# Four-layer convolution kernel: the sums of the last mixing's thresholded terms move from VectorE to GpSimd

## The chip, the core and the metric

The kernel runs on one core of one Trainium2 chip. The core has TensorE (PE in the profile), VectorE (DVE), ScalarE (ACT), GpSimd (POOL) and SyncE (SP), each with its own in-order stream of instructions, and a set of DMA engines fed by queues. The metric is the device time of one execution in microseconds (us).

## The reference

The input is four images of 64 channels of 256 x 256, all float32. Four layers follow each other. Layers 0, 1 and 3 convolve every channel with a filter that is a product of a row filter and a column filter, so that each is two products with Toeplitz matrices, and add `x * bias`. Layer 2 is the one that the change touches:

```python
f1 = haar2d(x)                                     # wavelet transform in both directions
for i in range(2):
    f4 = einsum('bchw,oc->bohw', f1 * v[i], conv_w[i])        # mixes the channels at each place
    acc = acc + sign(f4) * relu(abs(f4) - tau[i])             # a soft threshold
y = haar2d(acc, inverse=True) + x
```

## The kernel before, in words

For each image `b` the kernel runs layers 0 and 1 and the forward transform channel by channel (`convolutions`), then mixes the channels (`mixing`), then does the inverse transform and layer 3 channel by channel (`inverse`). The stages of one image are overlaid with those of the next. While the last image (b = 3) is mixed there is no next image; there the kernel does the layer 3 convolutions of 63 channels of the earlier images that were put off (`convolution`; their data come from the DRAM tensor `late`, and their steps carry the prefix "l").

The mixing of one image goes through 64 groups; a group holds 4 rows of the transform. Its steps, with their lines:

- `load` (L431, L435): a DMA fetches the group's coefficients `f`, and, for every fourth group, the scale factors `vt`.
- `mix` (L449): four matmuls (eight in the records) into `px` in PSUM.
- `scaled` (L468, VectorE) and `scaled_too` (L473, ScalarE): `f4 = px * v`. In the last mixing VectorE takes 8 of the 16 parts in one instruction, and ScalarE the other 8 one by one.
- `size` (L477, ScalarE): `mag = |f4|`. `sign` (L480, ScalarE): `f4 = sign(f4)`.
- `shrink` (L484, VectorE): `mag = mag - tau`. `signed` (L488, VectorE): `mag = max(mag, 0) * f4`.
- `add` (L494): two instructions, each of which adds the two terms i = 0, 1 of two of the rows and writes them into `z`, 256 elements for each of the 128 partitions.

`f4` and `mag` have two buffers each (pool `mx`, bufs=2). So L477 of group g + 2 overwrites what `add` of group g reads, and has to wait for it.

Two more kinds of work on VectorE lie in the same stretch. L292 is the sum at the end of a put-off convolution (`y = v * bias + product in PSUM`). L299 and L300 (`halve`, called by `level` and `butterfly`) are the levels of the inverse transform along one axis, done in place on `z`; the large ones take 128x1024 elements. A level needs the rows of `z` that it combines, and the channels 16 and up of `inverse` need the levels of their chunk of `z`.

The order on every engine is made when the program is built. Each step is put on a list with a due time (`at`, table `PLACE`), the list is sorted, and the framework then reorders instructions engine by engine by a cost model of its own, keeping the due times as priorities. An instruction whose inputs that model takes for ready can so be pulled ahead of others into what it takes for idle time. Waits between engines are semaphores set by the framework. On chip the order is fixed.

GpSimd does only one thing in this kernel: the short levels of the forward transform (L350 and L351 with lengths 32 to 2), 64 lots of ten instructions.

Of the kernel before, what the change touches and what calls it, by code (L numbers as in the profile page):

```python
# [16 lines left out]
B, C, S, EMB, ORD = 4, 64, 256, 33, 64  # L17
# [80 lines left out]
def conv_seq_kernel(ctx, tc, x, fz, fw, bias, decay, haar, haar_row, factors, vt, taut, wmix, out):  # L98
# [14 lines left out]
    nc = tc.nc  # L113
# [22 lines left out]
    z = zpool.tile([P, 4, P, 4, 16], F32, name="z")  # L136
# [182 lines left out]
    def at(time, run, unit):  # L319
        events.append((time, len(events), run, unit))  # L320
# [104 lines left out]
    def mixing(b, start, n_act):  # L425

        st = {}

        def load(g):
            f = mx.tile([P, 2, S], F32, name=f"f_{b}_{g}", tag="f", bufs=3)  # L430
            nc.sync.dma_start(f, coef[b].rearrange("k c p w -> (k c) p w")[:, 2 * g : 2 * g + 2])  # L431
            st[g] = {"f": f}
            if g % GT == 0:
                t = mx.tile([P, 2, GT, 16], F32, name=f"vt_{b}_{g}", tag="vt")
                nc.sync.dma_start(t, scales[g // GT])  # L435
                st["vt", g // GT] = t

        def scale(g, i):
            return st["vt", g // GT][:, i, g % GT, :]

        def over(g, i, n):
            return scale(g, i)[:, :n].unsqueeze(2).to_broadcast([P, n, C])

        def mix(g):
            f = st[g]["f"]
            ps = psx.tile([P, 2, 2, S], F32, name=f"px_{b}_{g}", tag="mix")
            for q in range(2):
                for h in range(2):
                    nc.tensor.matmul(  # L449
                        ps[:, q, h, :],  # L450
                        f[:, q, h * P : (h + 1) * P],
                        wb.rearrange("p r n -> p (r n)"),
                        start=True,
                        stop=True,
                    )
            if g == 0:

                one, two = ps[:, 0, :, :P], ps[:, 0, :, P:]
                d = mx.tile([P, 2, P], F32, name=f"d_{b}", tag="mag")
                nc.vector.tensor_copy(d, two)  # L460
                nc.vector.tensor_sub(two, one, d)
                nc.vector.tensor_add(one, one, d)
            st[g]["f4"] = mx.tile([P, 16, C], F32, name=f"f4_{b}_{g}", tag="f4")
            st[g]["px"] = ps.rearrange("p q h (r i o) -> p (q h r i) o", r=2, i=2)

        def scaled(g):
            px, n = st[g]["px"], 16 - n_act
            nc.vector.tensor_tensor(st[g]["f4"][:, :n], px[:, :n], over(g, 0, n), ALU.mult)  # L468

        def scaled_too(g, half):  # L470
            px, f4 = st[g]["px"], st[g]["f4"]
            for j in range(16 - n_act + half * (n_act // 2), 16 - (1 - half) * (n_act - n_act // 2)):
                nc.scalar.mul(f4[:, j], px[:, j], scale(g, 0)[:, j : j + 1])  # L473

        def size(g):
            mag = st[g]["mag"] = mx.tile([P, 16, C], F32, name=f"mag_{b}_{g}", tag="mag")
            nc.scalar.activation(mag, st[g]["f4"], AF.Abs)  # L477

        def sign(g):
            nc.scalar.activation(st[g]["f4"], st[g]["f4"], AF.Sign)  # L480

        def shrink(g):
            mag = st[g]["mag"]
            nc.vector.tensor_sub(mag, mag, over(g, 1, 16))  # L484

        def signed(g):
            mag = st[g]["mag"]
            nc.vector.scalar_tensor_tensor(mag, mag, 0.0, st[g]["f4"], ALU.max, ALU.mult)  # L488

        def add(g):  # L490
            parts = st.pop(g)["mag"].rearrange("p (q x i) (n c) -> p q i x n c", q=2, i=2, n=4)
            for q in range(2):
                to = slot(2 * g + q)
                nc.vector.tensor_add(  # L494
                    z[:, :, to].rearrange("p n x c -> p x n c"), parts[:, q, 0], parts[:, q, 1]
                )


        for g in range(S // 4):
            for name, stage in zip(  # L500
                ("mix load", "mix", "scaled", "scaled too", "scaled rest", "size", "sign", "shrink", "signed", "add"),
                (
                    load,
                    mix,
                    scaled,
                    lambda g: scaled_too(g, 0),
                    lambda g: scaled_too(g, 1),
                    size,
                    sign,
                    shrink,  # L510
                    signed,
                    add,
                ),
            ):
                at(start + g + PLACE[name if b + 1 < B else "l " + name], stage, g)
# [168 lines left out]
def slot(i):  # L684

    if i == 0:
        return 0
    n = 1 << i.bit_length() - 1
    return (2 * (i - n) + 1) * (P // 2 // n)
# [104 lines left out]
```

## Time and profile before

| What | us |
|---|---|
| median of 3 runs (lowest to highest) | 2875.76 (2874.41 to 2878.55) |
| the profiled execution | 2874.07 |
| its span in the trace | 2872.3 |
| PE busy | 2827.1 (98%) |
| DVE busy | 2494.9 (87%) |
| ACT busy | 2080.3 (72%) |
| POOL busy | 334.4 (12%) |

All times given as positions are from the start of the span. The last mixing's L488 instructions start between 2364.52 (group 0) and 2636.42 (group 63); GpSimd's last instruction starts at 2211.6. In a view in order of time a line gives the start, the time taken, engine, line, operation, output and inputs, size, and in brackets the engine's idle time before it with the instruction that ended it. The records of successive instructions of one engine overlap a little, so the time an instruction costs its engine is read from one start to the next.

### The profile page before, as it was taken

How to read it: one execution, taken by the hardware profiler on the slowest of the kernel's cores; microseconds unless marked ns; L12 is line 12 of the kernel's file. 1: busy time of each engine (PE TensorE's matmuls, PEld its weight loads, DVE VectorE, ACT ScalarE, POOL GpSimd, SP SyncE). 2: the span in 40 equal slices, each digit the busy share in tenths (PEclk: the TensorE clock that was granted, in tenths of full speed). 3: DMA queues.
4: the chain of work that ended last, by engine and by line, in shares of the span. 5: the costliest groups of instructions: out<-in, count | busy, mean ns of one | idle time of the engine just before them, and what ended most of it. 6: DMA issues, size and time to landing. Idle time of an engine off the chain costs nothing. (4 is left out here: it accounts for less than half of the span.)

```text
span 2872.3 us, 52434 instructions
## 1 busy us (share of the span) xinstructions
PE 2827.1 (98%) x16592; PEld 2555.6 (89%) x16592; DVE 2494.9 (87%) x4255; ACT 2080.3 (72%) x4950; POOL 334.4 (12%) x644
## 2 busy tenths in 40 slices
PE   9999999999999999999999999999999999999999
PEld 7899998898888898998898998998898998888998
DVE  4655558999999779999999779999999779999985
ACT  2333338999995558998985658999995659998554
POOL 0111111121121001221221001121121000000000
PEclk9999999999999999999999999999999999999999
DMA  6878787776667986777777986777777988787786
GB/s 182 249 231 230 232 232 227 207 208 204 205 209 213 289 254 198 214 213 214 209 207 236 299 255 196 213 214 216 208 208 235 297 266 235 229 238 212 224 241 201
DMA packets 599367, 649.77 MB, mean 226 GB/s; under 512 B 48465, under 2 KB 517044, under 8 KB 598964
## 3 DMA queue, kind: packets, MB, share of 16 engines
q1 hardware_dynamic: 536996, 578.61, 68.9%
q10 hardware_dynamic: 62096, 67.82, 6.7%
q8 instruction: 134, 2.20, 0.3%
q14 instruction: 141, 1.16, 0.1%
HBM read 426.77 MB, written 219.48 MB: 225 GB/s over the span
## 5 line engine op out<-in xcount | busy, mean ns | idle before, releaser
L261 PE MATMUL py<-t,a 128*128 128x256 f32 x3072 | 922.5, 382 | 9.5 <-ACT a L275 8.7
L275 ACT COPY a<-pa 128x512 f32<-128x512 f32 x768 | 478.8, 623 | 498.6 <-PE pa L262 455.2
L473 ACT ACTIVATE f<-px,vt 128x64 f32<-128x64 f32 x2816 | 610.5, 367 | 101.6 <-DVE f L468 101.1
L262 PEld LDWEIGHTS py<-t,a 128*128 128x128 f32 x3072 | 583.4, 190 | 79.3
L262 PE MATMUL py<-t,a 128*128 128x128 f32 x3072 | 590.0, 274 | 0.0
L261 PEld LDWEIGHTS py<-t,a 128*128 128x128 f32 x3072 | 497.3, 191 | 51.2 <-ACT a L275 19.0
L449 PE MATMUL px<-wb,f 128*128 128x256 f32 x2048 | 487.6, 380 | 7.6 <-ACT f L473 7.6
L449 PEld LDWEIGHTS px<-wb,f 128*128 128x128 f32 x2048 | 369.0, 190 | 50.0 <-ACT f L473 10.5
L351 POOL TENSOR_TENSOR sd<-less 128x128 f32<-128x128 f32 (+4 forms) x320 | 190.8, 596 | 1858.7 <-DVE less L350 1519.9
L534 ACT COPY zc<-z 128x512 f32<-128x512 f32 x256 | 282.1, 1105 | 108.1 <-PE pw L542 99.0
L484 DVE TENSOR_TENSOR mag<-mag,vt 128x1024 f32<-128x1024 f32 x256 | 316.6, 1237 | 12.3 <-ACT mag L477 11.5
L488 DVE SCALAR_TENSOR_TENSOR mag<-mag,f 128x1024 f32<-128x1024 f32 x256 | 316.6, 1238 | 0.0
L261 PE MATMUL pa<-t,y 128*128 128x256 f32 x1024 | 309.1, 384 | 6.8 <-DVE y L292 5.2
L261 PE MATMUL pa<-t,x 128*128 128x256 f32 x1024 | 305.9, 381 | 0.5 <-DMA t<-pad 0.5
L477 ACT ACTIVATE mag<-f 128x1024 f32<-128x1024 f32 x256 | 295.7, 1155 | 2.8 <-DVE z L494 0.4
L374 DVE TENSOR_TENSOR sp<-sd,sp 128x512 fp32r<-128x512 f32 x256 | 179.8, 702 | 129.3 <-ACT sp L369 128.2
L480 ACT ACTIVATE f<-f 128x1024 f32<-128x1024 f32 x256 | 285.8, 1116 | 3.5
L261 PE MATMUL pa<-t,u 128*128 128x256 f32 x772 | 233.2, 384 | 6.5 <-ACT w L548 2.8
L292 DVE SCALAR_TENSOR_TENSOR y<-x,bsb,py 128x512 f32<-128x512 f32 x256 | 190.9, 746 | 41.9 <-PE py L262 41.0
L262 PEld LDWEIGHTS pa<-t,x 128*128 128x128 f32 x1024 | 194.6, 190 | 26.3
L262 PEld LDWEIGHTS pa<-t,y 128*128 128x128 f32 x1024 | 194.5, 190 | 26.3
L292 DVE SCALAR_TENSOR_TENSOR y<-y,bsb,py 128x512 f32<-128x512 f32 x256 | 190.7, 745 | 26.0 <-PE py L262 25.6
(73 smaller groups left out, 4412.3 us busy)
## 6 DMA issues: line engine op xcount, KB each, us to landing
t<-pad SPq DMA_DIRECT2D x768, 256.0 KB, 4.1
x<-in_x SPq DMA_DIRECT2D x256, 256.0 KB, 3.7
coef<-co SPq DMA_DIRECT2D x256, 256.0 KB, 3.2
f<-coef SPq DMA_DIRECT2D x256, 256.0 KB, 3.2
r<-keep SPq DMA_DIRECT2D x256, 256.0 KB, 4.1
out_y<-y ACTq DMA_DIRECT2D x193, 256.0 KB, 4.3
keep<-sums SPq DMA_DIRECT2D x256, 128.0 KB, 2.8
keep<-sd SPq DMA_DIRECT2D x256, 128.0 KB, 2.8
```

The lines of the kernel that those rows point to most:

```text
L261: nc.tensor.matmul(ps[:, m, :], src[:, 0, m * P : (m + 1) * P], t[:, ::-1], start=True, stop=False)
L262: nc.tensor.matmul(ps[:, m, P:], src[:, 1, m * P : (m + 1) * P], t[:, : P - 1 : -1], start=False, stop=True)
L275: nc.scalar.copy(a, s["p" + new])
L292: nc.vector.scalar_tensor_tensor(y, s[res], bsb[:, layer, c : c + 1], s["p" + new], ALU.mult, ALU.add)
L351: engine.tensor_tensor(t[:, :, :, half:length], v[..., 0], v[..., 1], ALU.subtract)
L449: nc.tensor.matmul(ps[:, q, h, :], f[:, q, h * P : (h + 1) * P], wb.rearrange("p r n -> p (r n)"), start=True, stop=True,)
L473: nc.scalar.mul(f4[:, j], px[:, j], scale(g, 0)[:, j : j + 1])
L477: nc.scalar.activation(mag, st[g]["f4"], AF.Abs)
L480: nc.scalar.activation(st[g]["f4"], st[g]["f4"], AF.Sign)
L484: nc.vector.tensor_sub(mag, mag, over(g, 1, 16))
L488: nc.vector.scalar_tensor_tensor(mag, mag, 0.0, st[g]["f4"], ALU.max, ALU.mult)
L534: nc.scalar.copy(a.rearrange("p h k i -> p (h k) i"), z[:, c // 16, :, :, c % 16].rearrange("p i x -> p x i"))
```

## The change

In the last mixing (b = 3) GpSimd issues the two `add` instructions of groups 0 to 61; VectorE keeps those of groups 62 and 63, and all those of the other three mixings. The instructions, their operands and their due times stay the same.

```diff
             for q in range(2):
                 to = slot(2 * g + q)
-                nc.vector.tensor_add(
-                    z[:, :, to].rearrange("p n x c -> p x n c"), parts[:, q, 0], parts[:, q, 1]
-                )
+                engine = nc.gpsimd if b + 1 == B and g + 2 < S // 4 else nc.vector
+                engine.tensor_add(z[:, :, to].rearrange("p n x c -> p x n c"), parts[:, q, 0], parts[:, q, 1])
```

## The prediction

> **What bounds the kernel now.** I read the page first, then busy time by stretches of 20 us, then the engines in order of time inside the last mixing, the only stage that is changed.
>
> ```profile
> PE 2827.1 (98%) x16592; PEld 2555.6 (89%) x16592; DVE 2494.9 (87%) x4255; ACT 2080.3 (72%) x4950; POOL 334.4 (12%) x644
> POOL 0111111121121001221221001121121000000000
> ```
>
> TensorE is busy nearly throughout; the whole program leaves 45.2 us of its span idle (2872.3 - 2827.1). GpSimd has nothing in the last nine of the 40 slices, where the changed stage lies. The stretches (columns: window, length, busy time and records of PE, weight loads, DVE, ACT, POOL, then the granted clock and DMA):
>
> ```profile
> 2440.00:2460.00 20.00, 20.00 (x113) 18.12 (x112) 20.00 (x30) 19.56 (x54) 0.00 (x0) 1.00 0.86 256
> 2500.00:2520.00 20.00, 18.38 (x99) 16.27 (x98) 20.00 (x29) 18.87 (x50) 0.00 (x0) 1.00 0.70 214
> 2680.00:2700.00 20.00, 20.00 (x129) 18.43 (x128) 20.00 (x32) 11.97 (x17) 0.00 (x0) 1.00 0.71 210
> ```
>
> From 2440 on VectorE has no idle time at all (20.00 of 20), and TensorE and ScalarE have a little. So VectorE is the bound there, with the other two close behind. Before 2440 TensorE is full (20.00, 20.00 and 19.52 of 20 in the stretches that begin at 2360, 2400 and 2420). One group with a level, in order of time:
>
> ```profile
> 2503.93 0.80 DVE L494 TENSOR_TENSOR z<-mag 128x256 f32<-128x256 f32 x2
> 2504.60 1.27 DVE L488 SCALAR_TENSOR_TENSOR mag<-mag,f 128x1024 f32<-128x1024 f32 x1
> ...
> 2505.09 1.99 PE L449 MATMUL px<-wb,f 128*128 128x256 f32 x8 [1.61 <-ACT f L473]
> ...
> 2505.73 1.27 DVE L300 SCALAR_TENSOR_TENSOR z<-z 128x1024 f32<-128x1024 f32 x1
> ...
> 2506.87 0.73 DVE L468 TENSOR_TENSOR f<-px,vt 128x512 f32<-128x512 f32 x1
> ...
> 2507.47 1.26 DVE L484 TENSOR_TENSOR mag<-mag,vt 128x1024 f32<-128x1024 f32 x1
> ```
>
> Start to start this gives VectorE's prices: two adds 0.67, L488 1.13, a large level 1.14 (1.13 below), L468 0.60, L484 1.13 (to 2508.60); L292 takes 0.66 (2578.00 to 2578.66). A usual group is 0.66 + 0.60 + 1.13 + 0.67 + 1.13 = 4.19. TensorE's gap of 1.61 falls where a level is put in; there are five such places, at intervals of 8 or 9 groups.
>
> **The change part by part.** Removed from VectorE: 62 groups x 0.67 = 41.5 us. If nothing else moved, TensorE's idle time would be the limit of the gain. Its gaps from 2350 to the end of the mixing are 0.25, 0.23, 0.94, 1.61, 1.00, 1.17, 1.21, 1.29, 0.67, 0.67: 9.0 us; two more of 1.09 and 0.85 follow in the tail.
>
> But the listing of both programs' instruction orders shows that something else moves. The framework fills the time it thinks free on VectorE with levels (L299, L300) that stood behind the mixing. Between the first and the last L484 of the last mixing there were 5 large levels, and now there are 36; of the 128x512 ones 2 become 6. I count groups 16 to 61, from L488 of group 15 to that of group 61:
>
> - before: 46 x (1.13 + 0.60 + 1.13) + 40 x 0.66 + 46 x 0.67 + 5 x 1.13 + 0.60 = 195.0. The trace has 2628.16 - 2432.86 = 195.3, so the prices hold.
> - after: 46 x 2.86 + 41 x 0.66 + 36 x 1.13 = 199.3. VectorE has more to do in this stretch than before, 4.0 us over the 195.3, although the adds are gone.
>
> The levels are also uneven. Groups 55 to 59 hold six of them and cost 24.4, groups 21 to 23 hold none and cost 10.6. In the runs of groups that hold few levels TensorE and ScalarE set the pace: ScalarE is idle for 4.8 of the 180 us from 2440 to 2620, so of 195.3 / 46 = 4.25 a group it needs 4.14. Taking for each run of groups (16-20, 21-23, 24-29, 30-32, 33-41, 42-46, 47-50, 51-54, 55-59, 60-61) the larger of VectorE's sum and 4.14 a group: 23.7 + 12.4 + 27.2 + 12.4 + 38.9 + 21.5 + 17.5 + 16.6 + 24.4 + 8.3 = 202.9, so +7.6 rather than +4.0. Buffers two deep can't carry work over more than a group or two, so I take 7.6.
>
> **GpSimd's price.** The trace has no such add on GpSimd, but it has the same operation at other sizes, and it shows what VectorE does to it:
>
> ```profile
> 803.87 0.40 POOL L351 TENSOR_TENSOR sd<-less 128x128 f32<-128x128 f32 x1 [25.49 <-DVE less L350]
> ...
> 807.72 0.29 POOL L351 TENSOR_TENSOR sd<-less 128x64 f32<-128x64 f32 x1
> 807.97 4.93 POOL L350 TENSOR_TENSOR less<-less 128x32 f32<-128x32 f32 x1
> 812.86 0.23 POOL L351 TENSOR_TENSOR sd<-less 128x32 f32<-128x32 f32 x1
> ```
>
> ```profile
> 808.00 1.25 DVE L484 TENSOR_TENSOR mag<-mag,vt 128x1024 f32<-128x1024 f32 x1
> 809.13 0.79 DVE L494 TENSOR_TENSOR z<-mag 128x256 f32<-128x256 f32 x2
> 809.80 1.25 DVE L488 SCALAR_TENSOR_TENSOR mag<-mag,f 128x1024 f32<-128x1024 f32 x1
> 810.94 1.26 DVE L299 TENSOR_TENSOR z<-z 128x1024 f32<-128x1024 f32 x1
> 812.08 0.72 DVE L374 TENSOR_TENSOR sp<-sd,sp 128x512 fp32r<-128x512 f32 x1
> 812.68 0.78 DVE L292 SCALAR_TENSOR_TENSOR y<-x,bsb,py 128x512 f32<-128x512 f32 x1
> ```
>
> Left alone, 32, 64 and 128 elements take 0.23, 0.29 and 0.40 (0.45 in other lots), so 256 take 0.62 to 0.77; I take 0.70. The 4.93 is the same instruction that costs 0.23 two rows on: it stood still while VectorE ran instructions with two inputs in SBUF back to back, and ended just after L292, which reads PSUM, began. So GpSimd gets in beside L292 and L468, not beside L484, L488 or a level. The reverse shows too:
>
> ```profile
> 743.15 0.42 DVE L337 TENSOR_TENSOR sums<-y 128x256 f32<-128x256 f32 x1
> 743.49 0.62 DVE L338 TENSOR_TENSOR sd<-y 128x256 f32<-128x256 f32 x1
> ```
>
> L338 takes 0.55 to the next start where L337 takes 0.34, with a GpSimd instruction of 0.45 begun at 743.38. It was held to about 743.69, 0.14 before GpSimd's recorded end. I take 0.56 for what an add holds.
>
> A window of L292 and L468 together is 1.26. Two adds need 0.1 to start, 0.66 to the second's start and 0.56: 1.32, so VectorE loses about 0.05 a group, 46 x 0.05 = 2.3 us. If an add holds VectorE to its recorded end (0.70), it is about 0.2 a group, 9 us: the upper bound; the lower is 0. Windows are scarce: 46 + 41 for 92 adds. The order repeats the pattern "L484, L468, L488 | L292, L468, level, L484, level, L488" eight times (groups 25-26, 28-29, 33-34, 36-37, 42-43, 45-46, 51-52, and 54-55 with one level). By these prices, from the start of L488 of group 27: it ends at 1.13, L484 at 2.26; beside L468 (to 2.86) the first add of group 27 gets in and holds L488 of group 28 up to 2.92; that ends at 4.05. Beside L292 and L468 (to 5.31) go the second add of 27 and the first of 28. The second add of 28 then stands still through level, L484, level and L488, from 5.4 to 9.9, and ends at 10.65. On ScalarE, L477 of group 30 waits for it, ends at 11.8, and L484 of group 30, which could start at 11.2, starts at 11.9: 0.7 lost. Behind that L477 stand L480, the next group's L473s and an L275, and behind those TensorE's L449 and layer 3 products. 8 x 0.7 = 5.6 us. The lower bound is 0 (ScalarE catches up). The upper one: before, L477 of a group began 3.5 after L488 of the group two earlier ended (2510.54 to 2514.04), here 6.7, so ScalarE is 3.2 late; if all of that is lost, 26 us.
>
> The Trainium skill ("SBUF — State Buffer", section "Who interferes with whom") says that a VectorE instruction with two SBUF inputs and a GpSimd instruction that reads SBUF exclude each other, and that whichever began first keeps the port for its whole length. That speaks against this change; L338 agrees on the exclusion, but was released 0.14 before the recorded end. By the page's rule the sum has the upper bound of 9 us in place of 2.3, and the forecast is 7 us later; I go by the row.
>
> **What costs nothing.** No DMA is added or moved between queues; SP's stream has only neighbours swapped, at most a few places, and GpSimd's queue gets the adds behind its last lot, with nothing behind them. In groups 0 to 15 VectorE's sum falls from 70.2 to 64.6, but TensorE is full there: 0, at most -0.5. In groups 62 and 63 it falls by 0.7: I take -1. In the tail VectorE loses 31 large levels, yet TensorE is at 20.00 there while VectorE does them (the stretch from 2680): 0, at most -1.9.
>
> **Sum.** 7.6 + 2.3 + 5.6 - 1 = +14.5. With all bounds at their lower ends it is 4.0 - 0.5 - 1 - 1.9, about +1; with the upper ones 7.6 + 9 + 26 - 1, about +41. I keep the middle values since each comes from a walk through rows. The profiled execution took 2874.07 (span 2872.3 and 1.8 around it), 1.7 under the median. 2874.1 + 14.5 = 2888.6: 2889.
>
> **The rivals.**
> - *No loss beyond the order.* GpSimd's waits fall into VectorE's own idle time, and ScalarE catches up. The buffers spread the uneven levels, so that VectorE's average need (199.3 / 46 = 4.33 a group) sets the pace. For it: TensorE now loses only 0.9 to 1.6 at a level of 1.13 and closes up behind it. Against: two levels often stand in one group. Then +4.0 - 1 - 1.9, about +1: 2875.
> - *Faster.* VectorE stops being the bound, and TensorE closes its gaps: -11 at most, 2863. It decides if VectorE's work in groups 16 to 61 comes below 46 x 4.14 = 190.4; the count is 199.3, so its instructions would have to run 4.5% quicker without the adds. Nothing in the trace does so.
> - *GpSimd becomes the bound.* If an add usually stands through two instructions of 1.13 before it gets in, a group costs 2 x (2.26 + 0.66) = 5.84, 1.6 over the present pace: +98 for 62 groups; if a third of the groups do, +33: 2907 to 2972. For it: waits of 2 to 5 us are common in the present lots. Against: a wait stops ScalarE, then VectorE, and an idle VectorE lets GpSimd in.
>
> **How the numbers follow.** Three runs spread over 4 us, so a change within 0.2% (5.75 us) can't be told from none. Forecast (+6 to +41): 0.68. No loss: 0.17, within 0.2%. Faster: 0.06. GpSimd bound: 0.09. Slower is 0.68 + 0.09 = 0.77. The forecast's own range is 2880 to 2915. For 8 in 10 I go down to 2875, which takes in half of the second case, and up to 2915.
>
> **What would show it.** Right: VectorE still at 20.00 of 20 or stopped by ScalarE's L477; adds of 0.7 recorded where they meet L292 or L468, and of 2 us and more where they meet levels; TensorE's gaps in the mixing grow from 9 to about 23 us, ended by L473 and L275; the tail unchanged. Wrong: adds that overlap L484 or L488 at full speed; a mixing that is shorter; or levels that turn out to wait for adds.

## The result, and the profile after

| | before | after |
|---|---|---|
| median of 6 runs each (lowest to highest) | 2876.77 (2874.41 to 2880.05) | 2895.28 (2891.67 to 2897.36) |
| the profiled execution | 2874.07 | 2897.36 |
| its span | 2872.3 | 2895.6 |

The changed kernel takes 1.0061 of the time before (95% interval 1.0048 to 1.0074): 18.5 us more. Of the two profiled executions' 23.3 us, 6.4 lie before the changed stage: its first L449 starts at 2354.74 before and at 2361.14 after, and 5.2 of that is there already at the first mixing of the run (443.91 and 449.11), where both programs do the same work. From that L449 to the end it is 517.5 before and 534.4 after: +16.9. This is what the parts of the change have to explain. Each stretch here and below is read from one profiled execution; where programs do the same work it repeats closely (L488 of group 63 to the end: 233.1 in after, `small_adds` and `double_adds`, 236.8 in `levels_held`, `small_levels_held` and `half_held`).

| stretch, us (starts of L488) | before | after | difference | predicted |
|---|---|---|---|---|
| first L449 to L488 of group 0 | 9.8 | 9.8 | 0 | 0 |
| group 0 to 15 | 68.3 | 71.5 | +3.1 | 0 to -0.5 |
| group 15 to 61 | 195.3 | 212.5 | +17.2 | +15.5 |
| group 61 to 63 | 8.3 | 7.7 | -0.6 | -1 |
| group 63 to the end | 235.9 | 233.1 | -2.8 | 0 to -1.9 |

The page of after, busy time and GpSimd's slices:

```profile
PE 2835.4 (98%) x16592; PEld 2557.0 (88%) x16592; DVE 2470.6 (85%) x4131; ACT 2082.0 (72%) x4950; POOL 457.9 (16%) x768
POOL 0111111122121001211211001211211004443000
```

VectorE has 124 instructions fewer, yet its busy time falls only by 24.3 us, although the 124 sums took it 41.5: what is left got longer. The stretches of after (window, length, busy time and records of PE, weight loads, DVE, ACT, POOL, granted clock, DMA):

```profile
2440.00:2460.00 20.00, 18.43 (x98) 15.90 (x97) 18.89 (x20) 18.51 (x46) 7.68 (x10) 1.00 0.74 219
2500.00:2520.00 20.00, 18.37 (x97) 15.84 (x96) 19.60 (x21) 18.98 (x48) 10.06 (x10) 1.00 0.79 232
2680.00:2700.00 20.00, 20.00 (x130) 18.46 (x129) 14.96 (x29) 11.58 (x16) 0.00 (x0) 1.00 0.76 221
```

VectorE is still near full in the mixing, with 20 or 21 records where it had 29 or 30. TensorE has 18.4 of 20 in both stretches of the mixing, where it had 20.00 in the one and 18.38 in the other. In the tail (2680) VectorE has 5 us of room that it did not have, since levels are done already, and TensorE is full as before. VectorE of after in order of time, where two levels stand around an L484:

```profile
2503.67 0.73 DVE L292 SCALAR_TENSOR_TENSOR y<-v,bsb,py 128x512 f32<-128x512 f32 x1
2504.33 0.68 DVE L468 TENSOR_TENSOR f<-px,vt 128x512 f32<-128x512 f32 x1
2504.93 1.21 DVE L299 TENSOR_TENSOR z<-z 128x1024 f32<-128x1024 f32 x1
2506.07 1.75 DVE L484 TENSOR_TENSOR mag<-mag,vt 128x1024 f32<-128x1024 f32 x1
2507.74 1.21 DVE L300 SCALAR_TENSOR_TENSOR z<-z 128x1024 f32<-128x1024 f32 x1
2508.87 1.21 DVE L488 SCALAR_TENSOR_TENSOR mag<-mag,f 128x1024 f32<-128x1024 f32 x1
2510.01 0.73 DVE L292 SCALAR_TENSOR_TENSOR y<-v,bsb,py 128x512 f32<-128x512 f32 x1
2510.67 0.68 DVE L468 TENSOR_TENSOR f<-px,vt 128x512 f32<-128x512 f32 x1
2511.27 1.40 DVE L484 TENSOR_TENSOR mag<-mag,vt 128x1024 f32<-128x1024 f32 x1
```

GpSimd of after, the sums that meet them (L495 in this kernel; two in a line):

```profile
2504.30 2.43 POOL L495 TENSOR_TENSOR z<-mag 128x256 f32<-128x256 f32 x2
2510.16 1.43 POOL L495 TENSOR_TENSOR z<-mag 128x256 f32<-128x256 f32 x2 [3.43 <-DVE mag L488]
```

The pair begun at 2510.16 ends at 2511.59: 0.72 for each. It started beside L292 and L468 and reached 0.32 into L484, which is recorded with 1.40 in place of 1.21. The pair begun at 2504.30 ends at 2506.73. Its first sum fits beside L468; the second stands through the level L299 (2504.93 to 2506.07), gets in where L484 starts, and L484 costs 1.67 to the next start in place of 1.13, 0.54 more. L299 itself loses nothing, so the sum did not run beside it. The waits of after in the mixing, from 2340 to 2680 (engine, line, released by: us in total, times, longest):

```profile
PEld py L261 <- ACT a L275: 26.2, 28, 1.9
...
PE py L261 <- ACT a L275: 16.8, 19, 1.5
...
DVE z L299 <- POOL z L495: 5.3, 6, 1.6
```

The same window of before:

```profile
PEld py L261 <- ACT a L275: 4.8, 7, 1.5
```

TensorE now mostly waits for ScalarE's copy L275, and VectorE waits for GpSimd at six levels. ScalarE waits for no sum of GpSimd anywhere in this window.

### The profile page after: what moved, and what is told of

The parts are those of the page before. It is cut to its first block, busy times and chain, and to the rows that moved or that the text cites. A ratio compares the mean times of both kernels' runs of the same rounds, so it can differ in the third digit from the quotient of the medians.

```text
span 2895.6 us, 52462 instructions
## 1 busy us (share of the span) xinstructions
PE 2835.4 (98%) x16592; PEld 2557.0 (88%) x16592; DVE 2470.6 (85%) x4131; ACT 2082.0 (72%) x4950; POOL 457.9 (16%) x768
## 5 line engine op out<-in xcount | busy, mean ns | idle before, releaser
L275 ACT COPY a<-pa 128x512 f32<-128x512 f32 x768 | 479.3, 624 | 497.4 <-PE pa L262 451.1
L449 PE MATMUL px<-wb,f 128*128 128x256 f32 x2048 | 488.1, 380 | 8.3 <-ACT f L473 8.2
L449 PEld LDWEIGHTS px<-wb,f 128*128 128x128 f32 x2048 | 369.1, 190 | 51.5 <-ACT f L473 11.6
L484 DVE TENSOR_TENSOR mag<-mag,vt 128x1024 f32<-128x1024 f32 x256 | 320.9, 1254 | 14.2 <-ACT mag L477 13.3
L488 DVE SCALAR_TENSOR_TENSOR mag<-mag,f 128x1024 f32<-128x1024 f32 x256 | 312.4, 1221 | 0.8
L477 ACT ACTIVATE mag<-f 128x1024 f32<-128x1024 f32 x256 | 296.0, 1156 | 5.5 <-DVE z L495 0.4
L292 DVE SCALAR_TENSOR_TENSOR y<-x,bsb,py 128x512 f32<-128x512 f32 x256 | 190.1, 743 | 45.0 <-PE py L262 44.8
L292 DVE SCALAR_TENSOR_TENSOR y<-u,bsb,py 128x512 f32<-128x512 f32 x193 | 143.9, 746 | 85.1 <-PE py L262 83.3
```

Source lines behind the costliest of these rows:

```text
L275: nc.scalar.copy(a, s["p" + new])
L292: nc.vector.scalar_tensor_tensor(y, s[res], bsb[:, layer, c : c + 1], s["p" + new], ALU.mult, ALU.add)
L449: nc.tensor.matmul(ps[:, q, h, :], f[:, q, h * P : (h + 1) * P], wb.rearrange("p r n -> p (r n)"), start=True, stop=True,)
```

## The experiments

In all of them I read the stretch from L488 of group 15 to that of group 61 (195.3 before, 212.5 after; "the 46 groups") from the profile beside the time. VectorE's idle time is that between its records, ScalarE's prices are medians from one start to the next. Lines of code shift from kernel to kernel, so in the views of these runs a step is known best by its names (`mag<-mag,vt` is shrink, `z<-mag` a sum, `mag<-f` size, `f<-f` sign, `f<-px,vt` a scaled column).

### One cost taken alone: shorter sums, longer sums

`small_adds` keeps the changed kernel's order of instructions but for a few groups and shrinks the sums on GpSimd: each does 16 of its 256 elements and leaves the rest of `z` out.

```diff
+                out, one, two = z[:, :, to].rearrange("p n x c -> p x n c"), parts[:, q, 0], parts[:, q, 1]
+                if engine is nc.gpsimd:
+                    out, one, two = out[..., :1], one[..., :1], two[..., :1]
-                engine.tensor_add(z[:, :, to].rearrange("p n x c -> p x n c"), parts[:, q, 0], parts[:, q, 1])
+                engine.tensor_add(out, one, two)
```

> Each add on GpSimd does 16 of its 256 elements (every 16th channel of its rows) and leaves the rest out; the instruction order on VectorE is that of the changed kernel but for groups 4 to 7 and 20 to 23, with the same sums. Theory (the order of the levels costs some 7 us, and the adds' hold on VectorE's second input costs 8.5 us in L484): an add takes about 0.25 us instead of 0.73, L484 goes back from 1.32 to 1.14 us from start to start, and the kernel comes to 2885 us (2882 to 2889). Rival 1 (the order alone): 2893 to 2897, as the changed kernel. Rival 2 (the adds alone): 2873 to 2878, as before.

Measured: 2884.8, ratio 1.0031 (1.0021 to 1.0040). The 46 groups take 206.4 (2437.32 to 2643.73). With the same neighbours as above, VectorE of `small_adds`:

```profile
2502.86 0.68 DVE L468 TENSOR_TENSOR f<-px,vt 128x512 f32<-128x512 f32 x1
2503.46 1.21 DVE L484 TENSOR_TENSOR mag<-mag,vt 128x1024 f32<-128x1024 f32 x1
```

and GpSimd:

```profile
2502.36 0.45 POOL L498 TENSOR_TENSOR z<-mag 128x16 f32<-128x16 f32 x2 [5.35 <-DVE mag L488]
```

The pair takes 0.45 in place of 1.43, ends before L484 starts, and L484 is back at 1.21. So the new order costs 206.4 - 195.3 = 11.1 in the 46 groups, and what the full sums hold costs 212.5 - 206.4 = 6.1. The time is where it was expected; the split was expected at some 7 and 8.5. The 11.1 is that of the whole planned order: ScalarE's moved with VectorE's (before, its copy L275 stood between size and sign in 30 of the 46 groups, in after in 12). But VectorE is busy for 202.3 of the 206.4, 7.0 more than all of before's stretch, while ScalarE is idle for 14.4 and TensorE for 13.6, so most of it is VectorE's own work.

`double_adds` does every sum on GpSimd twice.

```diff
+                for _ in range(1 + (engine is nc.gpsimd)):
-                engine.tensor_add(z[:, :, to].rearrange("p n x c -> p x n c"), parts[:, q, 0], parts[:, q, 1])
+                    engine.tensor_add(z[:, :, to].rearrange("p n x c -> p x n c"), parts[:, q, 0], parts[:, q, 1])
```

> Each add on GpSimd is done twice; the instruction order on VectorE stays but for places in groups 1 to 6. Theory: the window beside L292 and L468 is full with two adds, so the two more of each group are paid by VectorE, some 1.3 us a group for 62 groups: 2975 us (2940 to 2990). Rival 1 (the order alone): 2895 us. Rival 2 (only the lateness of the adds counts, for the levels and for ScalarE): about 10 us more than the changed kernel, 2905.

Measured: 2955.5 in a single run, the 46 groups 262.6 (5.7 a group), VectorE idle for 28.9 of them. That lies in the expected range, but VectorE's instructions take only some 0.5 a group more than in after, where the theory had 1.3; the rest are waits. Of the kernel's waits from 2340 to 2740:

```profile
ACT mag L477 <- POOL z L496: 60.6, 42, 3.0
```

Now ScalarE's L477 does wait for the sums, 42 times. This is the third rival of the prediction (GpSimd as the bound, +33 to +98), and it needs about twice the work to come true.

### Groups 0 to 15: which side do they wait on?

`from16` leaves the sums of groups 0 to 15 on VectorE.

```diff
-                engine = nc.gpsimd if b + 1 == B and g + 2 < S // 4 else nc.vector
+                engine = nc.gpsimd if b + 1 == B and 16 <= g < S // 4 - 2 else nc.vector
```

> As the changed kernel, but VectorE keeps the sums of groups 0 to 15. Theory (the 3.1 us that groups 0 to 15 lost are small levels that stand behind sums on GpSimd): L488 of group 0 to that of group 15 takes 68.3 us as before in place of 71.5, with VectorE idle for under 1 us. The rival (they come from the order of the levels, or from TensorE): 71 us again. In groups 16 to 61 the listing gives VectorE 201.9 us where the changed kernel has 199.3, so I expect 213 to 215 us there; the time is then about 2894 either way, and by the rival 2897.

Measured: 2895.6, ratio 1.0064 (1.0047 to 1.0081). Groups 0 to 15 take 68.4, with VectorE idle for 0.4 where it was idle for 6.2 of the 71.5 in after. The waits of VectorE for GpSimd in that stretch of after

```profile
DVE z L299 <- POOL z L495: 3.9, 4, 1.6
```

are gone. The 46 groups take 213.1, at the lower end of what was expected, and the 3.1 us come back elsewhere: 0.6 there, 0.8 in groups 61 to 63, 1.7 in the tail. The kernel is no faster for it. Nor does `from16` separate the waits from the levels: it has 18 level instructions in groups 0 to 15, as before, where after has 28. `small_adds` tells more, as it has the 28 (its order differs in groups 4 to 7): it takes 68.6 there, and VectorE waits for GpSimd once, for 0.6. So the 3.1 us come with the full length of the sums: VectorE stands still at levels that the framework pulled to just behind the sums they need, and its instructions take 65.3 in place of 63.6.

### Without the levels: does the change then gain?

If the hoisted levels cost 11 us, keeping them behind the mixing should bring the gain back. `levels_held` adds a dependency: every level of the last image comes behind L488 of group 62. `hold_two` does so for the levels of chunks 2 and 3 alone.

```diff
-        nc.vector.tensor_sub(odd, even, odd)
+        step = nc.vector.tensor_sub(odd, even, odd)
+        if behind:
+            tc.add_manual_dep(step.ins, marks["signed"].ins.name, order, reason="levels stay behind the mixing")
...
-            at(tick + PLACE["level"], lambda _: level(n, chunk, *span), 0)
+            at(tick + PLACE["level"], lambda _: level(n, chunk, *span, behind=b + 1 == B), 0)
```

> The adds on GpSimd as in the changed kernel, but all levels of the last image are kept on VectorE behind L488 of group 62. Theory: VectorE's sum in groups 16 to 61 falls to 158 us and some 8 us of holds, below the 190.5 us that ScalarE and TensorE need, so the mixing is 5 us shorter than before and 22 us shorter than in the changed kernel; the tail gets 5 large levels more than before, 0 to 6 us: 2872 us (2866 to 2878). Rival 1 (GpSimd's adds themselves make the mixing late, through the two buffers of mag): over 2885 us. Rival 2 (the tail has no room for the levels, they bound it): over 2880 us, with TensorE's gaps behind 2640.

> As the one with all levels held, but the levels of chunk 1 of z are left free and only those of chunks 2 and 3 held. Theory: VectorE has 171.5 us and some 8 us of holds in groups 16 to 61, still under 190.5; the tail has 13 us less than with all levels held: 2868 us (2864 to 2874), faster than before. Rival 1 (the adds themselves are late): over 2885. Rival 2 (levels that wait for GpSimd's adds are what costs, wherever they are): 3 to 6 us above the one with all levels held.

Both missed: 2886.0, ratio 1.0034 (1.0022 to 1.0045), and 2886.5, ratio 1.0041 (1.0026 to 1.0057). The times are those of rival 1, but not its way: in neither trace does ScalarE's size wait for a sum of GpSimd. In `levels_held` the 46 groups take 201.5 although VectorE is idle for 22.5 of them; in `hold_two` 202.9, where VectorE waits for sums at nine of the levels left free, 8.0 us. The stretches of `levels_held` (columns as above) show no engine that is full; of 60 us TensorE has 56 to 58, ScalarE 56 to 57 and VectorE 53:

```profile
2440.00:2500.00 60.00, 58.06 (x315) 51.11 (x316) 53.38 (x55) 57.19 (x152) 19.91 (x28) 1.00 0.74 220
2500.00:2560.00 60.00, 56.13 (x296) 48.35 (x295) 52.89 (x53) 55.91 (x149) 19.49 (x28) 1.00 0.74 219
```

My explanation, that the levels alone stand in the way, was not enough. Three kernels look for the rest: `dve_levels_held` (the same hold, all sums on VectorE), `small_levels_held` (`levels_held` with the small sums from above; what its expectation calls VectorE's size and sign are L484 and L488) and `half_held` (GpSimd does only the first of the two sums).

```diff
+                engine = nc.gpsimd if b + 1 == B and g + 2 < S // 4 and q == 0 else nc.vector
```

> VectorE keeps all sums as in the kernel before, and the levels of the last image are held behind L488 of group 62, as in levels_held: the control for that run. From L488 of group 15 to that of group 61 VectorE has 46 x 2.86 + 40 x 0.66 + 46 x 0.67 = 188.8 us, and ScalarE needs about 4.14 x 46 = 190.4. Theory A (the sums on GpSimd are what made levels_held slow): 190 to 192 us in this stretch and a time of about 2871. Theory B (holding the levels changes the planned order so that ScalarE, TensorE and VectorE wait for each other in turn, whoever does the sums): about 200 us, as the 201.5 of levels_held, and a time of 2882 to 2887.

> As levels_held, but each sum on GpSimd does 16 of its 256 elements (the other 240 of z are left out), so that it takes about 0.25 us in place of 0.73. VectorE's order is that of levels_held. Theory A (what VectorE's size and sign instructions lose to full sums is what lengthens the stretch): 191 to 194 us from L488 of group 15 to that of group 61 in place of 201.5, a time of 2876 to 2879. Theory B (the order alone): 199 to 201 us, a time of 2883 to 2886.

> GpSimd does the first of each group's two sums, VectorE the second; the levels of the last image are held behind L488 of group 62. VectorE has 46 x 2.86 + 40 x 0.66 + 46 x 0.34 = 173.6 us in the stretch of 46 groups. Theory A (full sums on GpSimd cost VectorE and so the loop): about half of what levels_held lost, some 196 us and a time of 2880. Theory B (the order without levels): about 201 us and 2885.

| | sums of 62 groups | 46 groups | VectorE idle there | median | ratio (95%) |
|---|---|---|---|---|---|
| `dve_levels_held` | VectorE | 193.9 | 2.5 | 2877.6 | 1.0000 (0.9990 to 1.0009) |
| `levels_held` | GpSimd | 201.5 | 22.5 | 2886.0 | 1.0034 (1.0022 to 1.0045) |
| `small_levels_held` | GpSimd, 16 elements | 199.0 | 31.1 | 2882.0 | 1.0018 (1.0009 to 1.0028) |
| `half_held` | one of two each | 198.8 | 15.6 | 2879.4 | 1.0013 (1.0004 to 1.0023) |

Neither theory has all of it. Theory A is right that the control without GpSimd is faster (193.9), but its stretch was put 2 us and its time some 6.6 us too low. Theory B is right that tiny sums on GpSimd are nearly as slow as full ones (199.0): the full sums hold 2.5 us here, and 5.1 come from something else that moved. `half_held` has A's time, but in its stretch it lies between the two numbers that were to tell A from B, and decides nothing. Two orders moved. On VectorE, L292 stands behind L484 in 29 of the 46 groups of `levels_held`, and ahead of L468 in 34 of `dve_levels_held`. On ScalarE, the framework puts the copy L275 among the eight scaled columns or behind them; before, in 30 of the 46 groups, it stood between size and sign. The next runs take ScalarE's order as the suspect.

### ScalarE's order, pinned

`pinned` is `levels_held` with ScalarE's instructions of the last mixing chained by dependencies in the order of their due times, and the due times of the put-off product and its copy moved to 1.6 and 1.65. `dve_pinned` is the same with all sums on VectorE. In `pinned_copy_first` the product's due time stays and the copy's is 2.59.

```diff
+    def chain(step):
+        if "scalar" in marks:
+            tc.add_manual_dep(step.ins, marks["scalar"].ins.name, order, reason="ScalarE keeps the order of the due times")
+        marks["scalar"] = step
...
-    "l a3": 1.855,
-    "l a3 copy": 1.855,
+    "l a3": 1.6,
+    "l a3 copy": 1.65,
```

> As levels_held (GpSimd does the sums of 62 groups in full, all levels of the last image behind L488 of group 62), with ScalarE's instructions of the last mixing chained in the order size, sign, copy (L275), eight scaled columns, which is the order that dve_levels_held mostly had; in levels_held the copy stood between the scaled columns or behind them. Theory A (ScalarE's planned order is what costs levels_held its period of 4.38): from L488 of group 15 to that of group 61 between 190.4 (ScalarE's own need) and 196.4 (the 193.9 of dve_levels_held and 2.5 for what the full sums hold), a time of 2872 to 2880. Theory B (ScalarE's order matters little; VectorE's shrink instruction waits for the size of the same group because VectorE has too little to do in between): 199 to 202 us and 2884 to 2887.

> The control for pinned: the same chain on ScalarE and the same levels held, but VectorE does all sums. VectorE's sum is 188.8 us over the 46 groups. Theory A: 192 to 195 us and a time of 2876 to 2878, as dve_levels_held, since that had nearly this order. If this is slower than pinned, the sums are better on GpSimd once the order is mended; if it is faster, the full sums on GpSimd cost more than they free.

> As pinned, with the chain in the order copy (L275), size, sign, eight scaled columns, which is the order that the kernel before has in part of its groups. Theory A: 190.4 to 197 us from L488 of group 15 to that of group 61 and a time of 2872 to 2881, like pinned; should the place of the copy itself be what TensorE waits for, this is slower than pinned by the 1.06 to 2.1 us that the copy stands later or earlier in some groups, up to 201 us and 2886. Theory B: 199 to 202 us in both.

| | 46 groups | median | ratio (95%) |
|---|---|---|---|
| `pinned` | 199.2 | 2881.1 | 1.0018 (1.0009 to 1.0027) |
| `dve_pinned` | 200.0 | 2882.6 | 1.0018 (1.0008 to 1.0028) |
| `pinned_copy_first` | 204.4 | 2890.2 | 1.0047 (1.0032 to 1.0062) |

Theory A's numbers missed in all three, though the trace shows why for `pinned`. One premise was wrong at the outset: `dve_levels_held` has the order size, sign, copy in only 16 of its 46 groups, and in about as many the copy stands between size and sign. ScalarE of `pinned` in order of time:

```profile
2500.07 1.06 ACT L490 ACTIVATE mag<-f 128x1024 f32<-128x1024 f32 x1
2501.16 1.06 ACT L495 ACTIVATE f<-f 128x1024 f32<-128x1024 f32 x1
2502.13 0.57 ACT L275 COPY a<-pa 128x512 f32<-128x512 f32 x1
2502.59 1.76 ACT L484 ACTIVATE f<-px,vt 128x64 f32<-128x64 f32 x8
2504.44 1.06 ACT L490 ACTIVATE mag<-f 128x1024 f32<-128x1024 f32 x1
```

There is no wait for another engine in this group: it is ScalarE's own 4.37. I had taken 4.14 as its need. But an instruction that has to wait for the one just before it on ScalarE starts later than one that has not. Sign overwrites the `f4` that size reads, and size reads what the last column writes; in the trace both wait for a semaphore that ScalarE itself raises, and the copy does not. Size to sign is 1.089, size to copy 0.963; a last column to size 0.457, column to column 0.197. The order decides how often ScalarE pays this: 1.089 + 0.964 + 0.466 + 7 x 0.197 + 0.457 = 4.355 a group here, and 0.965 + 0.465 + 0.959 + 7 x 0.196 + 0.396 = 4.16 in the order that 30 groups of the kernel before have.

`dve_pinned`, the same order, is as slow for a different mixture: ScalarE needs less there (a last column to size is 0.396), but its columns start 4.4 us later than the prices give, 2.9 of it put down to VectorE's `scaled`. What makes `pinned_copy_first` slow is not settled: TensorE's `px` waits for ScalarE's columns (11.2 us) and VectorE's `scaled` for `px` (10.0 us), but TensorE's order differs from that of `pinned` too, with the products of the put-off channels exchanged (they stand as in before and in `levels_held`).

`pinned_between` tests the reading of `pinned` by one step. The copy goes between size and sign. TensorE's order stays; VectorE's does not, other than the expectation says: L292 stands right behind L488 in 24 of the 46 groups of `pinned`, and behind L484 in 40 of `pinned_between`.

```diff
-    "l a3 copy": 1.65,
+    "l a3 copy": 1.61,
```

> As pinned, with one thing moved: on ScalarE the copy (L275) stands between size and sign, as in 30 of the 46 groups of the kernel before; the orders of TensorE and VectorE are those of pinned. Theory (ScalarE itself is the bound in pinned, because its instructions stand back to back on their own results): start to start pinned has size 1.089, sign 0.964, copy 0.466, seven columns of 0.197 and a last one of 0.457, together 4.355 a group with a copy and 3.89 without; with the copy in between, size takes 0.963 in place of 1.089, 4.23 a group. Over 41 groups with a copy that is 5.2 us less: 193 to 195 us from L488 of group 15 to that of group 61 in place of 199.2, and a time of 2875 to 2877, equal to the kernel before. Rival (another wait, such as VectorE's shrink for size or TensorE's for the copy, takes over): 198 to 200 us and 2880 to 2882. Should it come below 2873, the sums on GpSimd beat the kernel before once the order is mended.

Measured: 2878.0, ratio 1.0003 (0.9994 to 1.0012), the 46 groups 193.1. ScalarE of `pinned_between`:

```profile
2501.47 1.06 ACT L490 ACTIVATE mag<-f 128x1024 f32<-128x1024 f32 x1
2502.44 0.57 ACT L275 COPY a<-pa 128x512 f32<-128x512 f32 x1
2502.90 1.06 ACT L495 ACTIVATE f<-f 128x1024 f32<-128x1024 f32 x1
2503.86 1.74 ACT L484 ACTIVATE f<-px,vt 128x64 f32<-128x64 f32 x8
```

The copy starts 0.97 after size, and sign 0.96 before the columns: the 1.09 is gone. The stretch is 6.0 shorter than in `pinned`, where 41 x (4.355 - 4.223) = 5.4 were worked out from the prices; the medians differ by 3.2. That VectorE's order moved too leaves the reading standing: ScalarE's own prices fill 198.0 of the 199.2 in `pinned` and 192.5 of the 193.1 here, and they are the same in the other runs, whatever VectorE's order (size to copy 0.963 to 0.965, size to sign 1.089 to 1.093 wherever no other wait comes in between). So with the levels held and ScalarE's order restored, the full sums on GpSimd come out even with the kernel before, not ahead of it: VectorE is idle for 13.7 us of the 46 groups, and ScalarE's own prices (41 x 4.223 + 5 x 3.88 = 192.5) are the bound. No kernel here beats the one before. For `levels_held` itself the account isn't closed: ScalarE's prices sum to about 194 in its order, and the other 7.5 us are waits between the engines, of which 5.5 (2440 to 2620) are ScalarE's for `scaled`; the edit of `pinned` also moved `scaled` and the place of L292 on VectorE, and exchanged the products of the put-off channels on TensorE, so its gain over `levels_held` isn't the copy's alone. The place of L292 by itself does not make a kernel slow, as `pinned_between` shows.

## Why the prediction was right, and where it was not

The forecast was 2889 in a range of 2875 to 2915, slower with 0.77; it is 2895.3, slower. The sum of +14.5 compares with +16.9 between the traces. The closeness is partly luck: the term for the order was 3.5 too low and that for groups 0 to 15 was 3.1 too low, while the two terms for GpSimd's sums, 7.9 together, stand against a measured 6.1, and the tail gained 2.8 that the sum did not count on. The terms one by one:

- **The order of the levels and their unevenness, +7.6.** Right in kind, too small: `small_adds` puts the whole new order at 11.1, ScalarE's part of it included. In that run VectorE's instructions take 202.3 where I counted 199.3 (steps of 0.1 and less at many places, not taken apart), and it is idle for 4.1, where I had allowed 3.6 for groups with few levels.
- **What the sums hold, +2.3.** The mechanism was right: a sum gets in beside L292 and L468, which read PSUM, and holds what follows to about 0.13 before its own recorded end (L338 in the trace of before gave 0.14). The price was too low, and the place was incomplete. Two sums of 0.72, begun 0.15 after L292, reach 0.32 beyond the window of 1.26; L484 behind it lost 0.19 to 0.27 in each of 18 groups, 3.7 in all, where I had 0.05 a group. And L484 lost 0.54 to 0.62 in each of eight places behind a level, 4.4. Together it is L484 that grew: 60.6 us after, 52.1 before, 53.2 in `small_adds`.
- **The second sum that stands still and makes ScalarE late, +5.6.** This step failed. I let a sum starve through level, L484, level and L488, as L350 had in the trace of before. No sum of after takes longer than 1.79, its own 0.73 and the rest of one VectorE instruction; the median is 0.73. ScalarE's L477 never waits for one in the mixing of after; it does, 42 times, when the sums are done twice (`double_adds`). In the same eight patterns GpSimd got in at the first boundary, ahead of L484, and VectorE paid directly. In place of the 5.6 that I booked on ScalarE stand the 4.4 above, on VectorE.
- **Groups 0 to 15 at nothing.** Failed: +3.1. I said TensorE is full there and looked only at VectorE's sum, which falls. The text named "levels that turn out to wait for adds" as a sign of being wrong, and that is what the waits of after and the shorter sums of `small_adds` show; `from16` won the 3.1 back in that stretch and lost it again behind it.
- **Groups 62 and 63, -1; the tail, at most -1.9.** Measured -0.6 and -2.8.
- **Signs.** TensorE's gaps in the mixing were to grow from 9 to about 23; they sum to 23.5, mostly ended by L275 and L449's wait on ScalarE. Sums of 2 us and more did not occur. VectorE was to stay at 20.00 of 20 or be stopped by L477; it is at 18.89 and 19.60 in the stretches shown.

The rival "no loss beyond the order" underrated the order itself: `small_adds`, the nearest to it, is at 2884.8 and not at 2875. The rival "faster" was priced by ScalarE's 4.14 a group. That number belongs to the order before, and `levels_held` and `pinned` show that a new plan can take it away while VectorE rests.

The Trainium skill ("SBUF — State Buffer", section "SBUF: two separate sides") says that whichever of a two-input VectorE instruction and a GpSimd instruction began first keeps the port for its whole length. The trace agrees that they exclude each other, down to the sum that waits through L299. The page does not say where in a record that length ends. Taken to the recorded end of the sum, L484 would have lost 0.66 in the example behind a level and 0.32 in the other pattern; it lost 0.54 and 0.19, so the hold ended 0.12 to 0.13 earlier.

## What to carry to other kernels

Before moving work off a full engine, look at the order the program gets, not only at the diff: here the freed time was filled with other work, pulled forward to where it is not hidden. In `pinned`, with that work held back, a second engine was the bound, by an order that no longer hid the starts that wait for its own preceding instruction. A step on GpSimd that reads SBUF can be paid by VectorE where VectorE's next instruction has two SBUF inputs (here L484 lost 0.19 to 0.62 in 26 of 46 groups), so compare the length of the windows with the length of the step first. When an engine looks relieved and the period doesn't fall, sum the start-to-start times of the next engine in its new order before looking for a wait.

## What the hardware showed that I had not expected

- ScalarE pays where an instruction waits for the one just before it: 0.13 from size to sign, and 0.20 to 0.26 from the last column to size, against what an independent successor costs. In `pinned_between` the copy starts 0.09 before size's recorded end (2502.53), in `pinned` sign starts 0.03 after it (2501.13). The Trainium skill ("Perfetto Trace Analysis", section "DVE / Act Engine Instruction") has a record end with the acknowledged write while the next instruction may begin earlier; the independent pairs here agree with that.
- A last column to size takes 0.457 where GpSimd does full or tiny sums and 0.396 where VectorE does them (`levels_held` and `small_levels_held` against `dve_levels_held`), some 2.5 us over 41 groups. One difference goes with it in the records: where VectorE does the sums, size itself waits for ScalarE's last column and starts 0.03 after its recorded end; where GpSimd does them, size waits for GpSimd, the wait for the column stands in an instruction of its own ahead of it, and size starts 0.09 after that end. No run takes this apart.
- GpSimd got in at the first boundary between two VectorE instructions with two SBUF inputs in all eight patterns of after, while the one at 807.97 of the trace of before stood for 4.93 us, through all such instructions up to L292. What decides this stays open; no run was made for it.
